# Attention weights summed over four steps in both halves, and the second feed-forward product taken transposed

## The chip, the cores and the metric

The kernel runs on one core of a Trainium2 chip. Time is the device time of one execution in microseconds. Five runs of the kernel before gave 4252.23 to 4266.6 us, with a median of 4262.65 us. A profile is one further execution, recorded instruction by instruction. The engines are TensorE (PE; its weight loads are PEld), VectorE (DVE), ScalarE (ACT), GpSimd (POOL) and SyncE (SP). SP and POOL issue the DMA transfers.

## The reference

Sixteen graphs of 1024 nodes with 256 features pass through four layers, in float32. The graphs share one adjacency matrix. Every layer normalizes its input, clips it at zero, applies a graph layer and adds the result to the input. Layers 0 to 2 are graph attention with 4, 1 and 1 heads. Layer 3 is self-attention with 8 heads of 32 features, masked by the adjacency, followed by a norm, a feed-forward part of two products, and another norm:

```python
attn = softmax(where(mask, q @ k.T / sqrt(32), -1e9))
t = attn @ v
x = layernorm(x + t, ln1_g, ln1_b)
h = relu(x @ w1 + b1)
x = layernorm(x + (h @ w2 + b2), ln2_g, ln2_b)
```

The change touches layer 3 alone: the row sums of the softmax, and the second product.

## The kernel before

**Plan.** `direct` (L301) does the work. Each operation is recorded with its engine, a cost in microseconds, and the buffers that it reads and writes. `Record.schedule` (L170) then runs a list scheduler over the whole program: at each turn it takes the operation that can start earliest, and among those that are ready the one with the smallest key. What comes out is the fixed order of each engine's queue and of the DMA queues of SP and POOL. The hardware follows it with semaphores. The key of an operation is its batch number plus a value read off a curve for its stage (`GATS` for the three graph layers, `VALUES` for the projections of layer 3, `STEPS` for its attention, `FEED` for the feed-forward part), less `LEAD` for ACT and DVE. `BIAS` weighs PE's switching between kinds of matmul. With these curves several batches are in work at once: the feed-forward part of one batch, the attention of a second and the graph layers of later ones are woven into each other. In the steady part a batch takes some 258 us (starts of the scores of batches 4 to 14 in the trace).

**Attention of layer 3** (`attention`, L1029). For each of two head groups `g` (four heads each) and each half `hf` of the query nodes (512 columns) there are eight steps `jt`, one per 128 key nodes. A step computes the scores of four heads on PE (L1297) into the `sc` ring of four PSUM banks, takes the exponential on ACT (L1321) into two tiles `pa` of 1024 columns, and multiplies these by the mask on DVE (L1330). Two steps later (`LAG`) PE multiplies them with the values in a `quad`: four heads side by side, 32 columns each (L1163, `pa,va`). The softmax sums come from another quad with a tile of ones (`sums,ones` or `pa,ones`).

To save quads, the weights of several steps are first added. `run_of` (L1171) says how many: one in the last batch; otherwise four in half 1 and two in half 0. In a run, the second step's tiles are added to the first's by DVE into `sums` (L1190). The third and fourth step's tiles are added into `sums` by DMAs that accumulate, issued on POOL's queue (L1198). `sums` is a ring of two tiles, that is one run at a time; `pa` is a ring of six tiles, that is three steps.

**Projections of queries and keys** (`project`, L1072). Eight times a batch, PE forms a product in an `sc` bank (L1079), ACT copies it rounded to `hi` (L1088), DVE subtracts to get `lo` (L1091), and SP issues 16 DMAs of 64 KB that stack copies of `hi` and `lo` into `qs` or `ks` (L1100). `hi` and `lo` exist once each, so the next projection's copy waits until these DMAs have read them. The table `later` places the projections at steps 0, 2 and 4 of certain halves; those of group 1's first queries and keys are in half 1 of group 0.

**Feed-forward part** (`feed`, L1343), per half: `turn` takes the first norm's statistics on DVE, normalizes `hna` on ACT, transposes it on PE and applies scale and shift on the way out of PSUM (`yT`, ACT L1382). It also scales and shifts the untransposed `hna` on DVE with rows on all partitions (L1397). `forward` forms the first product transposed (L1406) and its relu on ACT into `fz` (L1427). `back`, two node tiles at a time, forms the second product straight, with the weights `w2` moving (L1463); DVE adds `hna` while leaving PSUM and also yields the row sums (L1475, into `z`). Then follow the squares on ACT (L430), a power on POOL (L450), and the scaling and the addition of the layer's input on DVE (L1500, L1513). The result is stored by SP.

**PSUM.** Four banks are the `sc` ring. The other four (`r_bank`) are shared by all else and given out by the plan.

Of the kernel before, what the change touches and what calls it, by code (L numbers as in the profile page):

```python
# [22 lines left out]
P = 128  # L23
# [9 lines left out]
def rows_on_all(ap, n):  # L33

    return bass.AP(tensor=ap.tensor, offset=ap.offset, ap=[[0, P], [1, n]])
# [222 lines left out]


LANDING = 2.8  # L260
BIAS = 1.211
LEAD = {"act": 2.365, "dve": 1.821}

SWITCH = {
    ("full", "col4"): 0.095,
# [16 lines left out]
def tt_us(n):  # L282
    return (n / 0.96 + 73) / 1000


def stt_us(n):
    return (n / 0.96 + 130) / 1000
# [6 lines left out]
def mm_us(n):  # L294
    return 2 * max(2 * n / 2.4 + 2.3, 109) / 1000
# [5 lines left out]
def direct(ctx, tc, flag, x, adj, gat_w, gat_a, w_qkv, ln1_g, ln1_b, ln2_g, ln2_b, w1, b1, w2, b2, out):  # L301
# [9 lines left out]
    HG = P // D3  # L311

    GATS = (
        (-4.564, -3.715, -2.378, -1.791, -0.286),
        (-0.159, 0.648, 0.672, 0.678, 0.719),
        (0.713, 0.729, 0.86, 0.888, 1.159),
    )
    VALUES = (0.885, -0.207, 0.784, 0.867, 1.288)
    STEPS = (0.767, 1.497, 1.58, 1.837, 1.895)
    FEED = (3.303, 2.616, 2.682, 3.025, 3.186)  # L320

    const = ctx.enter_context(tc.tile_pool(name="const", bufs=1))
    ident = const.tile([P, P], F32, name="ident")
# [15 lines left out]
    w1_sb = const.tile([P, CT, C], F32, name="w1_sb")  # L339
    w2_sb = const.tile([P, CT, C], F32, name="w2_sb")  # L340

    cols = {n: const.tile([P, CT], F32, name=f"col_{n}") for n in ("b1", "g1", "c1")}
    rows = {n: const.tile([P, 1, C], F32, name=f"row_{n}") for n in ("g1", "cb", "g2", "c2")}
    mask = const.tile([P, NT, N], U8, name="mask")

    least = const.tile([P, NT], F32, name="least")
# [5 lines left out]
    def ring(name, n, shape, pool=work):  # L352
        return Ring([pool.tile([P] + shape, F32, name=f"{name}{i}") for i in range(n)])
# [24 lines left out]
    r_reca = ring("reca", 1, [CT * 2 * TH * HG])  # L378
    r_mv1 = ring("mv1", 2, [NT, 2])
    r_rstd1 = ring("rstd1", 2, [NT])  # L380
    r_yT = ring("yT", 1, [CT, HALF])
    r_fz = ring("fz", 2, [HALF])
    r_z = ring("z", 2, [HALF])
    r_sums = ring("sums", 2, [2, HALF])
    r_mvz = ring("mvz", 2, [2, 2])
    r_rstdz = ring("rstdz", 2, [2])
# [15 lines left out]
    def pe(us, emit, w, r, modes=("full", "full")):  # L402
        rec.add("pe", us, emit, w, r, modes)
# [4 lines left out]
    def dve(us, emit, w, r):  # L408
        rec.add("dve", us, emit, w, r)
# [233 lines left out]
    def setup():  # L643
        rec.stream(-3.0, (0.0, 1.0), False)
        prepare(0)
        rec.stream(-0.9, (0.0, 0.1), False)
        for it in range(NT):
            neighbours(it)
        rec.stream(-0.5, (0.0, 0.3), False)
        prepare(1)  # L650
        prepare(2)
        dma(
            3.2,
            lambda: nc.sync.dma_start(wqkv_sb, w_qkv.rearrange("(t p) d -> p t d", p=P)),
            [b_qkv],
            [],
        )

        def load_feed():
            nc.sync.dma_start(w1_sb, w1.rearrange("(t p) d -> p t d", p=P))  # L660
            nc.sync.dma_start(w2_sb, w2.rearrange("(t p) d -> p t d", p=P))
            for n, ap in (("b1", b1), ("g1", ln1_g), ("c1", ln1_b)):
                nc.sync.dma_start(cols[n], ap.rearrange("(t p) -> p t", p=P))
            for n, ap in (("g1", ln1_g), ("cb", ln1_b), ("g2", ln2_g), ("c2", ln2_b)):
                nc.sync.dma_start(rows[n][:, 0, :], rows_on_all(ap, C))
            nc.gpsimd.dma_start(rows["cb"][:, 0, :], rows_on_all(b2, C), accum_op=ALU.add)

        dma(5.0, load_feed, [b_feed], [], us=3.6)

# [359 lines left out]
    def attention(b, xt, b_mv, b_rstd):  # L1029
# [140 lines left out]

        def run_of(g, hf):  # L1171

            return 1 if b == NB - 1 else 4 if hf == 1 else 2

        rec.stream(b, STEPS)
        GROUP = 2
# [166 lines left out]
    def feed(b, x3, hn):  # L1343

        mv, rstd = r_mv1.new(), r_rstd1.new()
        yTs, fTs = {}, {}

        def turn(hf):
            s = slice(hf * TH, (hf + 1) * TH)
            its = range(hf * TH, (hf + 1) * TH)  # L1350
            for it in its:
                stats(hn.at(it), hn(it), mv.t[:, it, :], mv(it), "f")
            mv_refs = [mv(it) for it in its]
            inverse(mv.t[:, s, 0], mv.t[:, s, 1], rstd.t[:, s], mv_refs, rstd(hf))
            for it in its:
                u = hn.at(it)
                normal(
                    u,
                    hn(it),
                    u,  # L1360
                    hn(it),
                    mv.t[:, it, 0:1],
                    rstd.t[:, it : it + 1],
                    [mv(it), rstd(hf)],
                    AF.Identity,
                )
            yTs[hf] = r_yT.new()
            for ct in range(CT):
                g = r_bank.new()
                pe(  # L1370
                    0.109 * TH,
                    lambda: transposes(
                        lambda k: g.t[:, k * P : (k + 1) * P],
                        lambda k: hn.half(hf)[:, k, ct * P : (ct + 1) * P],
                        TH,
                    ),
                    [g, yTs[hf](ct)],
                    [hn(it) for it in its],
                )
                act(  # L1380
                    act_us(HALF, 2),
                    lambda: nc.scalar.activation(  # L1382
                        yTs[hf].t[:, ct, :],
                        g.t,
                        AF.Identity,
                        bias=cols["c1"][:, ct : ct + 1],
                        scale=cols["g1"][:, ct : ct + 1],
                    ),
                    [yTs[hf](ct)],
                    [g, b_feed],  # L1390
                )

            h = hn.half(hf)
            for op, row in ((ALU.mult, "g1"), (ALU.add, "cb")):
                dve(
                    tt_us(TH * C),
                    lambda: nc.vector.tensor_tensor(  # L1397
                        h, h, rows[row].to_broadcast([P, TH, C]), op
                    ),
                    [hn(it) for it in its],  # L1400
                    [b_feed],
                )

        def product(g, co, w_sb, src):
            for ct in range(CT):
                nc.tensor.matmul(  # L1406
                    g.t,
                    w_sb[:, ct, co * P : (co + 1) * P],
                    src(ct),
                    start=ct == 0,  # L1410
                    stop=ct == CT - 1,
                )

        def forward(hf):
            yT = yTs[hf]
            fT = fTs[hf] = [r_fz.new() for _ in range(CT)]
            for co in range(CT):
                g = r_bank.new()
                pe(
                    CT * mm_us(HALF),  # L1420
                    lambda: product(g, co, w1_sb, lambda ct: yT.t[:, ct, :]),
                    [g, fT[co]],
                    [yT],
                )
                act(
                    act_us(HALF, 1),
                    lambda: nc.scalar.activation(  # L1427
                        fT[co].t, g.t, AF.Relu, bias=cols["b1"][:, co : co + 1]
                    ),
                    [fT[co]],  # L1430
                    [g],
                )

        def back(hf):
            fT = fTs[hf]
            for it in (hf * TH, hf * TH + 2):
                g, z, mvz, rstdz = r_bank.new(), r_z.new(), r_mvz.new(), r_rstdz.new()
                xr = r_xr.new()
                dma(
                    1.15,  # L1440
# [15 lines left out]
                def pz():  # L1456
                    return g.t.rearrange("p (t c) -> p t c", c=C)

                def product2():
                    for k in range(2):  # L1460
                        i0 = (it % TH + k) * P
                        for ct in range(CT):
                            nc.tensor.matmul(  # L1463
                                pz()[:, k, :],
                                fT[ct].t[:, i0 : i0 + P],
                                w2_sb[:, ct, :],
                                start=ct == 0,
                                stop=ct == CT - 1,
                            )

                pe(2 * CT * mm_us(C), product2, [g], fT)
                for k in range(2):
                    dve(
                        stt_us(C) + 0.03,
                        lambda: nc.vector.scalar_tensor_tensor(  # L1475
                            z_t[:, k, :],
                            pz()[:, k, :],
                            0.0,
                            hn.at(it + k),
                            op0=ALU.add,  # L1480
                            op1=ALU.add,
                            accum_out=mvz.t[:, k, 0:1],
                        ),
                        [z(k), mvz(k)],
                        [g, hn(it + k)],
                    )
                refs = [mvz(0), mvz(1)]
                spread_of(
# [712 lines left out]
```

## Time and profile before

| | before |
|---|---|
| median of 5 runs | 4262.65 us |
| profiled execution | 4254.21 us, span 4252.4 us |
| PE matmul busy | 4086.5 us, 96% |
| DVE busy | 3565.4 us, 84% |
| ACT busy | 2659.8 us, 63% |
| POOL busy | 628.2 us, 15% |
| mean granted PE clock | 0.986 |
| accumulating DMAs `sums<-pa` | 240, 512 KB, 5.9 us from issue to landing (median) |
| projection DMAs to `qs` and `ks` | 2048, 64 KB, 2.0 to 2.1 us |

A group's row in the profile reads: line, engine, operation, output and inputs by the program's names, shapes and count; after the first bar busy time and mean duration in ns; after the second the time its engine stood idle just before, and for whom. A wait reads: who waited for whom, microseconds in total, times, the longest. The chain is the sequence of work that ended last, followed back from the end of the program; its rows give each engine's share of the span. SPq and POOLq are the queues from which DMAs are issued. In a timeline row the first two numbers are start and duration in us. A busy PE is in matmuls whose ends are modelled, so its busy time contains some overlap.

### The profile page before, as it was taken

Reading aid. Unit: us, or ns where it says so; the run is one execution under the profiler, and the core shown is the slowest. Engines: PE = TensorE matmul, PEld = TensorE weight load, DVE = VectorE, ACT = ScalarE, POOL = GpSimd, SP = SyncE. Lnnn points to the kernel's source line nnn. Section 1 sums busy time; section 2 is a strip of 40 time slices with the busy share of each in tenths; the row PEclk is TensorE's granted clock in tenths of the full one; section 3 lists DMA queues with packets and bytes.
Section 4 is the critical chain, followed back from the end, with each engine's and each line's share of the span. In section 5 each row is a group of like instructions: output and inputs, shape, how many; then the busy total and the mean of one; then the engine's idle time right before and its main releaser. Section 6 shows DMA issues by size and latency. Waiting matters only on the chain.

```text
span 4252.4 us, 68427 instructions
## 1 busy us (share of the span) xinstructions
PE 4086.5 (96%) x23874; PEld 2397.1 (56%) x23874; DVE 3565.4 (84%) x6266; ACT 2659.8 (63%) x6383; POOL 628.2 (15%) x632
## 2 busy tenths in 40 slices
PE   7999999999999999999999999999999999999998
PEld 3746556465564645656465564645646456564653
DVE  7487887988889888897988889888898888979877
ACT  3556657665675756657566576666757566575665
POOL 0001111111111111111111111111111111111110
PEclk9999999999999999999999999999999999999999
DMA  3123443343443434443244433334434344332442
GB/s 106 33 67 85 120 98 91 77 97 100 100 104 78 99 84 97 112 93 94 68 99 119 102 87 84 90 102 97 106 74 98 87 97 112 88 89 70 97 113 53
DMA packets 215410, 390.05 MB, mean 92 GB/s; under 512 B 44945, under 2 KB 80401, under 8 KB 215057
## 3 DMA queue, kind: packets, MB, share of 16 engines
q1 hardware_dynamic: 180352, 259.62, 21.8%
q0 software_dynamic: 34704, 125.98, 16.0%
q8 instruction: 191, 3.13, 0.3%
q14 instruction: 163, 1.33, 0.1%
HBM read 91.43 MB, written 33.95 MB: 29 GB/s over the span
## 4 chain that ended last, share of the span: by engine, by line
PE 43%; DVE 20%; ACT 10%; SPq 8%; DMA 6%; issue 4%; POOL 1%; DVEq 0%; ACTq 0%; POOLq 0%
PE bank L842 14%; PE bank L1163 8%; SPq L1100 8%; DVE pt L815 8%; PE sc L1297 6%; DVE pa L1330 5%; PE bank L718 4%; ACT pa L1321 3%; DVE sums L1190 2%; PE bank L513 2%; PE sc L1079 2%; ACT waste L430 2%; PE bank L929 2%; DMA qs<-lo 1%; DMA xt<-in_x_dram 1%
## 5 line engine op out<-in xcount | busy, mean ns | idle before, releaser
L1321 ACT ACTIVATE pa<-sc 128x512 f32<-128x512 f32 x2048 | 1108.7, 602 | 519.0 <-PE sc L1297 323.3
L1330 DVE TENSOR_TENSOR pa<-pa,mask 128x1024 f32<-128x1024 f32 x1024 | 1223.0, 1216 | 97.5 <-ACT pa L1321 94.1
L815 DVE SCALAR_TENSOR_TENSOR pt<-row,e,mask 128x512 f32<-128x512 f32 x1536 | 1063.1, 740 | 33.7 <-DMA row<-rd 24.3
L842 PE MATMUL bank<-qb,pt 128*128 128x257 f32 x4096 | 965.6, 387 | 1.5 <-ACT ex L870 1.0
L842 PEld LDWEIGHTS bank<-qb,pt 128*128 128x128 f32 x4096 | 784.0, 193 | 164.0 <-issue 37.4
L1297 PE MATMUL sc<-qs,ks 128*128 128x512 f32 x2048 | 736.8, 463 | 58.3 <-DVE lo L1091 55.6
L1163 PE MATMUL bank<-pa,va 128*32 128x512 f32 x4096 | 525.4, 597 | 0.7 <-DVE pa L1330 0.7
L1297 PEld LDWEIGHTS sc<-qs,ks 128*128 128x128 f32 x2048 | 368.6, 192 | 273.2 <-ACT pa L1321 74.4
L929 PE MATMUL bank<-pt,qb 128*32 128x512 f32 x4096 | 510.2, 596 | 5.4 <-DVE pt L815 5.4
L1190 DVE TENSOR_TENSOR sums<-pa,pa 128x1024 f32<-128x1024 f32 x360 | 431.0, 1212 | 25.6 <-PE bank L1163 25.5
L718 PE MATMUL bank<-w_aug,hT 128*128 128x259 f32 (+1 forms) x1536 | 390.6, 395 | 2.9 <-ACT hT L712 2.0
L718 PEld LDWEIGHTS bank<-w_aug,hT 128*128 128x128 f32 x1536 | 283.6, 192 | 118.1 <-issue 17.4
L1198 POOL DMA_DIRECT2D sums<-pa x240 | 209.9, 875 | 949.1 <-DVE xt L895 295.2
L929 PEld LDWEIGHTS bank<-pt,qb 128*32 128x32 f32 x4096 | 131.1, 109 | 298.4 <-issue 208.1
L939 PE MATMUL bank<-pt,e 128*32 128x512 f32 x2048 | 285.8, 594 | 0.0
L1163 PEld LDWEIGHTS bank<-pa,va 128*32 128x32 f32 x4096 | 123.8, 109 | 269.9 <-issue 227.7
L870 ACT ACTIVATE ex<-bank,rec 128x256 f32<-128x256 f32 x256 | 120.9, 472 | 209.9 <-DVE rec L862 209.8
L1079 PE MATMUL sc<-hTa,wqkv_sb 128*128 128x512 f32 x512 | 243.7, 604 | 2.1 <-ACT pa L1321 1.9
L484 ACT ACTIVATE hn<-xt,mv,rstd 128x256 f32<-128x256 f32 x384 | 207.7, 609 | 47.1 <-DVE mv L474 31.9
L450 POOL TENSOR_TENSOR rstd<-rstd,neg_half 128x4 f32<-128x4 f32 x94 | 118.0, 1256 | 702.4 <-DVE rstd L442 662.5
L1163 PE MATMUL bank<-sums,ones 128*32 128x512 f32 x1440 | 205.3, 603 | 3.6 <-ACT ex L870 1.9
L430 ACT ACTIVATE waste<-xt,mv 128x256 f32<-128x256 f32 x376 | 191.5, 509 | 9.5
(119 smaller groups left out, 4302.2 us busy)
## 6 DMA issues: line engine op xcount, KB each, us to landing
sums<-pa POOLq DMA_DIRECT2D x240, 512.0 KB, 5.9
row<-rd SPq DMA_DIRECT2D x192, 256.0 KB, 3.2
ks<-hi SPq DMA_DIRECT2D x512, 64.0 KB, 2.1
ks<-lo SPq DMA_DIRECT2D x512, 64.0 KB, 2.0
qs<-hi SPq DMA_DIRECT2D x512, 64.0 KB, 2.0
qs<-lo SPq DMA_DIRECT2D x512, 64.0 KB, 2.0
xt<-in_x_dram SPq DMA_DIRECT2D x32, 512.0 KB, 4.8
x<-xt SPq DMA_DIRECT2D x32, 512.0 KB, 3.2
```

What stands on the lines that cost most here:

```text
L718: nc.tensor.matmul(g.t[:, : C + 3 * H], hT.t[:, ct, k * P : (k + 1) * P], w_aug[l][:, ct, :], start=ct == 0, stop=ct == CT - 1,)
L815: lambda: nc.vector.scalar_tensor_tensor(pt.t, row.t, e3[:, 2, jt // TH, h, jt % TH : jt % TH + 1], mask[:, jt, hf * HALF : (hf + 1) * HAL ...
L842: nc.tensor.matmul(g.t[:, : D + 1], pts[jt].t[:, k * P : (k + 1) * P], qb[:, jt, 0, :], start=jt == 0, stop=jt == NT - 1,)
L929: nc.tensor.matmul(g.t[u * D + d : u * D + d + D3, :], qb[:, j, h + u, d : d + D3], pts[u][j - jt].t, start=j == 0, stop=j == NT - 1,)
L939: nc.tensor.matmul(gd.t[c : c + D3, :], one(jt + k, h + u).to_broadcast([P, D3]), pts[u][k].t, start=jt == 0, stop=jt == NT - 2,)
L1079: nc.tensor.matmul(sc.t, wqkv_sb[:, ct, c0 : c0 + P], hT.t[:, ct, hf * HALF : (hf + 1) * HALF], start=ct == 0, stop=ct == CT - 1,)
L1100: lambda: nc.sync.dma_start(stack.t[a * D3 : (a + 1) * D3, r, at : at + HALF], part.t[r * D3 : (r + 1) * D3, :],),
L1163: nc.tensor.matmul(ac.t[r * D3 : (r + 1) * D3, :], columns(r), of_head(r), start=first, stop=last,)
L1190: lambda: nc.vector.tensor_add(ss.t, p0.t, p1.t),
L1297: nc.tensor.matmul(scs[r - r0].t, ks.t[:, r, jt * P : (jt + 1) * P].bitcast(F32R), q.t[:, r, :].bitcast(F32R), start=True, stop=True,)
L1321: lambda: nc.scalar.activation(pt.t[:, v, :], sc.t, AF.Exp, scale=1.0 / math.sqrt(D3)),
L1330: lambda: nc.vector.tensor_mul(pt.t, pt.t, mask[:, jt : jt + 1, i0 : i0 + HALF].to_broadcast([P, 2, HALF]),),
```

## The change

The sums of the softmax are taken over runs of four steps in both halves. In the feed-forward part the second product is formed transposed, like the first: `w2` is the stationary operand and 512 columns of `fz` move. DVE adds the bias and `yT` while leaving PSUM, back into `yT`. `back` then transposes two node tiles at a time on PE, and ACT copies them from PSUM to `z` and yields the row sums. The untransposed `hna` is no longer scaled and shifted and no longer read by `back`. `yT` gets two buffers, `fz` three, and `z` uses `fz`'s. The rows `g1` and `cb` with their loads go, a column `b2` comes. All numbers of the plan (`BIAS`, `LEAD`, `GATS`, `VALUES`, `STEPS`, `FEED`) are others.

```diff
-BIAS = 1.211
-LEAD = {"act": 2.365, "dve": 1.821}
+BIAS = 1.132
+LEAD = {"act": 2.934, "dve": -1.486}
...
     GATS = (
-        (-4.564, -3.715, -2.378, -1.791, -0.286),
-        (-0.159, 0.648, 0.672, 0.678, 0.719),
-        (0.713, 0.729, 0.86, 0.888, 1.159),
+        (-4.712, -3.106, -1.99, -1.162, 0.152),
+        (0.067, 0.407, 0.645, 0.73, 0.787),
+        (0.795, 0.852, 0.847, 0.891, 1.302),
     )
-    VALUES = (0.885, -0.207, 0.784, 0.867, 1.288)
-    STEPS = (0.767, 1.497, 1.58, 1.837, 1.895)
-    FEED = (3.303, 2.616, 2.682, 3.025, 3.186)
+    VALUES = (0.829, 0.292, 0.735, 1.372, 1.153)
+    STEPS = (1.102, 1.337, 1.602, 1.943, 1.949)
+    FEED = (2.285, 2.308, 2.405, 2.48, 2.233)
...
-    r_yT = ring("yT", 1, [CT, HALF])
-    r_fz = ring("fz", 2, [HALF])
-    r_z = ring("z", 2, [HALF])
+    r_yT = ring("yT", 2, [CT, HALF])
+    r_fz = ring("fz", 3, [HALF])
...
-            for n, ap in (("b1", b1), ("g1", ln1_g), ("c1", ln1_b)):
+            for n, ap in (("b1", b1), ("b2", b2), ("g1", ln1_g), ("c1", ln1_b)):
...
-            for n, ap in (("g1", ln1_g), ("cb", ln1_b), ("g2", ln2_g), ("c2", ln2_b)):
+            for n, ap in (("g2", ln2_g), ("c2", ln2_b)):
...
-            nc.gpsimd.dma_start(rows["cb"][:, 0, :], rows_on_all(b2, C), accum_op=ALU.add)
...
-            return 1 if b == NB - 1 else 4 if hf == 1 else 2
+            return 1 if b == NB - 1 else 4
...
-            h = hn.half(hf)
-            for op, row in ((ALU.mult, "g1"), (ALU.add, "cb")):
-                dve(
-                    tt_us(TH * C),
-                    lambda: nc.vector.tensor_tensor(
-                        h, h, rows[row].to_broadcast([P, TH, C]), op
-                    ),
...
         def forward(hf):
...
+            for co in range(CT):
+                g = r_bank.new()
+                pe(
+                    CT * mm_us(HALF),
+                    lambda: product(g, co, w2_sb, lambda ct: fT[ct].t),
+                    [g],
+                    fT,
+                )
+                u = yT.t[:, co, :]
+                dve(
+                    stt_us(HALF),
+                    lambda: nc.vector.scalar_tensor_tensor(
+                        u, g.t, cols["b2"][:, co : co + 1], u, op0=ALU.add, op1=ALU.add
+                    ),
+                    [yT(co)],
+                    [g],
+                )
...
-                def product2():
+                def turn_back():
                     for k in range(2):
                         i0 = (it % TH + k) * P
-                        for ct in range(CT):
-                            nc.tensor.matmul(
-                                pz()[:, k, :],
-                                fT[ct].t[:, i0 : i0 + P],
-                                w2_sb[:, ct, :],
...
+                        transposes(
+                            lambda ct: pz()[:, k, ct * P : (ct + 1) * P],
+                            lambda ct: yT.t[:, ct, i0 : i0 + P],
+                            CT,
+                        )
...
-                pe(2 * CT * mm_us(C), product2, [g], fT)
+                pe(0.109 * 2 * CT, turn_back, [g], [yT])
                 for k in range(2):
-                    dve(
-                        stt_us(C) + 0.03,
-                        lambda: nc.vector.scalar_tensor_tensor(
...
+                    act(
+                        act_us(C) + 190e-3,
+                        lambda: nc.scalar.activation(
+                            z_t[:, k, :], pz()[:, k, :], AF.Copy, accum_out=mvz.t[:, k, 0:1]
+                        ),
                         [z(k), mvz(k)],
-                        [g, hn(it + k)],
+                        [g],
                     )
```

## The prediction

> **What bounds the kernel now.** I read the page first (busy shares, chain, queues), then the groups by line, then who waits for whom, and last the timeline around the longest wait of TensorE (PE). The profiled execution took 4254.2 us: a span of 4252.4 and 1.8 around it. It lies 8.4 us below the median of the five runs, 4262.65; sums are made on 4254.2, and 8.4 is added at the end. A difference under 0.2% (8.5 us) can't be told from no change here.
>
> ```profile
> PE 4086.5 (96%) x23874; PEld 2397.1 (56%) x23874; DVE 3565.4 (84%) x6266; ACT 2659.8 (63%) x6383; POOL 628.2 (15%) x632
> q1 hardware_dynamic: 180352, 259.62, 21.8%
> q0 software_dynamic: 34704, 125.98, 16.0%
> PE 43%; DVE 20%; ACT 10%; SPq 8%; DMA 6%; issue 4%; POOL 1%; DVEq 0%; ACTq 0%; POOLq 0%
> ```
>
> PE is busy 96%, so its work sets the time, but only 43% of the chain is PE. VectorE (DVE, 84%) and the transfers with their issue (SPq and DMA, 14% together) break in. Queue q0 holds the accumulating DMAs.
>
> ```profile
> L1163 PE MATMUL bank<-sums,ones 128*32 128x512 f32 x1440 | 205.3, 603 | 3.6 <-ACT ex L870 1.9 <-DMA sums<-pa 1.4
> L1190 DVE TENSOR_TENSOR sums<-pa,pa 128x1024 f32<-128x1024 f32 x360 | 431.0, 1212 | 25.6 <-PE bank L1163 25.5
> L1198 POOL DMA_DIRECT2D sums<-pa x240 | 209.9, 875 | 949.1 <-DVE xt L895 295.2 <-DVE reca L1257 168.7 <-DVE sums L1190 122.4
> L1463 PE MATMUL bank<-w_sb,fz 128*128 128x256 f32 x512 | 121.7, 386 | 12.8 <-ACT fz L1427 12.8
> L1406 PE MATMUL bank<-yT,w_sb 128*128 128x512 f32 x256 | 119.7, 593 | 1.3 <-ACT yT L1382 1.3
> L513 PE MATMUL bank<-ident,hn 128*128 128x128 f32 x768 | 116.7, 285 | 12.6 <-ACT hn L484 10.4 <-DVE rec L985 1.0
> L1557 ACT ACTIVATE waste<-xt 128x256 f32<-128x256 f32 x120 | 50.6, 421 | 20.6 <-DMA xt<-in_x_dram 18.8
> ```
>
> These rows are the prices. 1440 matmuls are 180 sums of four heads (8 records each). The accumulating DMAs hardly hold PE: 1.4 us. They act elsewhere:
>
> ```profile
> PE sc L1297 <- DVE lo L1091: 55.6, 17, 6.4
> DVE lo L1091 <- DMA qs<-lo: 48.8, 12, 6.4
> ACT pa L1321 <- DVE sums L1190: 126.3, 60, 5.0
> ACT pa L1321 <- DMA sums<-pa: 7.1, 6, 2.3
> ```
>
> PE's largest wait, 55.6 us in 17 times (about one in each batch), is for `lo`, the low part of a query or key projection, and `lo` waits for the transfers that still read the one `lo` buffer. The timeline of one batch shows why they are late:
>
> ```profile
> 2077.51 4.94 SPq L1100 DMA_DIRECT2D qs<-lo  x8
> ```
> ```profile
> 2128.37 8.21 SPq L1100 DMA_DIRECT2D qs<-lo  x8
> ...
> 2129.26 0.92 POOL L1198 DMA_DIRECT2D sums<-pa  x1 [16.02 <-DVE ota L1264]
> ...
> 2130.61 0.87 POOL L1198 DMA_DIRECT2D sums<-pa  x1
> ...
> 2135.19 0.86 POOL L1198 DMA_DIRECT2D sums<-pa  x1 [3.71 <-DVE pt L815]
> ...
> 2141.88 0.50 PE L1297 MATMUL sc<-qs,ks 128*128 128x512 f32 x1 [3.96 <-DVE lo L1091]
> ```
>
> The same eight issues of SP take 4.94 us with no accumulating DMA about, and 8.21 us when three start during them. Then `lo` is freed late, its subtraction waits at the head of DVE's queue, the score bank it reads stays taken, and PE stands still for 3.96 us.
>
> **The change part by part.**
>
> *Sums of four steps in the first half too.* In 15 batches and 2 head groups, half 0 goes from 4 runs of two to 2 runs of four. PE loses 60 of 180 sums. Four quads back to back last 3.57 us in the chain (0.89 each); busy time gives 205.3/180 = 1.14. So -53.5 to -68; I take -53.5, because a removed quad frees what it occupies between neighbours.
> DVE loses 120 of 360 adds: 120 x 1.212 = -145 us of work. Most lies beside PE. L1190 holds 2% of the chain, some 90 us; a third of it is 30. Bounds 0 to -31; I take -10, since PE itself waits only 0.7 us for masked weights (`pa`). ACT's 126 us of waits for these adds lie in its idle 37%.
> POOL gains 240 x 0.875 = +210 us of issue (15% to 20%). Each issue waits for masked weights; behind it in POOL's queue stand the powers for the norms (L450, L465), for which DVE waits 39.1 + 24.1 + 12.0 = 75 us now. Doubled, and with DVE's 20% of the chain, +15 at most, 0 at least; I take +3, as most of these waits are near the power's own 1 us.
> The landing (5.9 us) must precede the sum; the 1.4 us above price that at 0 to +2, cover being the other groups' products that PE runs meanwhile. If that cover is gone, each of 60 runs would show up to 5.9.
>
> *The transfers.* Accumulating DMAs go from 240 to 480 of 512 KB, q0 from 16% to 32%. SP issues what it issued before in every batch, 128 projection pieces included. The last two steps' accumulations of a run are issued two steps on, so those of half 0's second run start in the first steps of half 1, where queries and keys of the next head group are projected and where PE already stalls. There, eight issues that today pass undisturbed (the `hi` part) would lengthen by the 3.3 us seen above. I price one more stall of today's size in each batch: 15 x 55.6/17 = +49 us. Bounds: 0, if SP issues nothing in the new windows, and +98 for two places. I take +49: of the trace's rows this place is the nearest.
> A rule of the Trainium skill is to be held against this ("DMA: Bandwidth & Descriptors", section "Issuing engines are not separate DMA queues"): DMAs of SP, ACT and POOL end on the same 16 engines and interleave, so POOL's queue is no second road. It speaks against the change and with the 8.21 us. The same page's fit for a POOL DMA ("Anatomy of one DMA") makes 512 KB an estimated 3.2 us; the trace has 5.9, and the trace decides. By 3.2 the disturbance would be 3.2/5.9 of +49, some +27.
>
> *The second feed-forward product, transposed.* PE: 512 matmuls of 256 columns (121.7) become 256 of 512 columns, the shape of L1406 (119.7): -2. Added: 16 transposes per batch, 256 in all. 768 like them are busy 116.7 us (0.152 each, +39); eight in a row in the chain take 0.87 to 1.04 (+28 to +33). I take +36, bounds +28 to +42.
> DVE: 64 scale and shift operations go (39.1 + 38.8 = -78), 128 sums with accumulation go (50.9 + 10.4 = -61), 64 fused adds of 512 from PSUM come. The trace has none; bounds are 0.68 (a product of 512 from PSUM, L992) and 0.74 (L815), so +45. With the adds, DVE falls by some 239 us to 78%. I credit no more than the -10 above: PE does not wait for L1397 or L1475.
> ACT: 128 copies with accumulation, 0.421 + 0.197 each (L1557), +79 us, 63% to 65%. Its idle time hides them; with ACT's 10% of the chain +8 at most.
> At the very end, where nothing covers the feed-forward part, a product (1.7), a fused add (0.7), transposes (0.4) and a slower copy come in, and 2.4 of scale and shift and the straight product (0.9 to 1.7) go: 0, within 3. Setup loads lose a POOL DMA and two broadcasts and gain a small column: 0, hidden by the adjacency work of the first 240 us, within 2.
>
> *Rings and the plan's numbers.* `yT` 2, `fz` 3, `z` gone: 0; PE waits 14 us in all for these tiles. `BIAS`, `LEAD`, `GATS` and the rest reorder everything. No row prices that. A better order can win at most PE's idle time between start and tail: 165.9 less 42 (first 240 us), 17 (last 142 us) and 55.6 for `lo` is 51. I set the loss equally: -51 to +51, taken as 0.
>
> Sum: -53.5 - 10 + 3 + 49 + 36 - 2 = +22.5. 4254.2 + 22.5 = 4276.7; with 8.4, 4285.
>
> **Rivals.**
> *PE's work decides (faster).* The new accumulations fall where SP issues nothing: the +49 is gone, -26.5, 4236. For it: of the present windows only one place per batch stops PE, and half 0's first run could fall between projections. Against: projections follow each other in SP's queue with hardly a gap around that place. It decides from 26 us, about half a stall per batch.
> *Two stalls or a worse order.* Another place of the same kind, or an order that costs +51: 4334 to 4336. For it: q0 at 32% also meets the row broadcasts and the x loads, which are in the chain today. Against: DVE at 78% has more slack.
> *Half of it.* SP's slowing costs about 1.6 us per batch: 4285 - 25 = 4260, no change. For it: the two DMAs of a step overlap.
> *The change doesn't do what it says:* the sums go, but each run ends in a wait for the landing, 60 x 5.9 x one half = +177. Half 1 does the same now and PE waits 1.4 us, so 2 in 100, inside the slower cases.
>
> **How the numbers follow.** Forecast (4285, own range 4268 to 4310) 0.40; two stalls or a worse order 0.20; PE's work decides 0.28; half of it 0.12. Of the forecast's 0.40 some 0.02 lies within 0.2%, of "half" 0.09 does and 0.03 is faster. Faster 0.31, same 0.11, slower 0.58. The range reaches to the faster case with half of the order's gain (4236 - 25, 4210) and to the worse case with a little over (4348).
>
> **What would show it.** After: 960 sum records for `sums` instead of 1440, 240 adds, 480 accumulating DMAs; DVE near 78%, q0 near 32%; PE's waits for `lo` near 105 us instead of 55.6, with SP's issues of `qs` and `ks` longer. The forecast is wrong if `lo` waits stay at 55 or fall: then the time is near 4236. It is also wrong if PE's longest wait is for landed sums, or if PE's busy time does not fall by about 20.

## The result, and the profile after

The changed kernel takes 4247.11 us (median; 4236.88 to 4253.29), the kernel before 4255.4 us over all its runs. The ratio is 0.998, with a 95% interval of 0.9975 to 0.9985: some 8 us faster, at the edge of what can be told here. The forecast was 4285, slower. The time lies inside the range, but the sign was wrong. The profiled execution took 4248.12 us, with a span of 4246.3.

From the page of the changed kernel: busy times and the DMA queues.

```profile
PE 4094.9 (96%) x23394; PEld 2348.6 (55%) x23394; DVE 3373.0 (79%) x5890; ACT 2669.4 (63%) x6639; POOL 788.3 (19%) x871
q0 software_dynamic: 69120, 251.69, 31.4%
q1 hardware_dynamic: 180336, 259.36, 21.6%
```

DVE's busy time fell by 192 us and POOL's rose by 160 us; q0 doubled. PE's busy time *rose* by 8 us. The groups (count; busy and mean; idle before) show why, first the value quads (`pa,va`) of the kernel before, then the changed kernel:

```profile
L1163 PE MATMUL bank<-pa,va 128*32 128x512 f32 x4096 | 525.4, 597 | 0.7 <-DVE pa L1330 0.7
```
```profile
L1161 PE MATMUL bank<-pa,va 128*32 128x512 f32 x4096 | 584.2, 601 | 28.8 <-DVE pa L1328 25.4 <-DVE yT L1430 3.1
L1196 POOL DMA_DIRECT2D sums<-pa x480 | 420.4, 877 | 1540.3 <-DVE pa L1328 533.3 <-DVE sums L1188 188.8 <-PE sc L1295 153.7
L1188 DVE TENSOR_TENSOR sums<-pa,pa 128x1024 f32<-128x1024 f32 x240 | 288.6, 1217 | 29.4 <-PE bank L1161 27.2
L1161 PE MATMUL bank<-sums,ones 128*32 128x512 f32 x960 | 147.7, 603 | 3.4 <-DMA sums<-pa 3.4
L1392 PE MATMUL bank<-fz,w_sb 128*128 128x512 f32 x256 | 124.7, 610 | 0.6 <-ACT fz L1413 0.6
L512 PE MATMUL bank<-ident,yT 128*128 128x128 f32 x256 | 40.6, 283 | 6.6 <-DVE yT L1430 4.1 <-ACT yT L1379 2.4
```

The sums fell from 205.3 to 147.7, the new transposes take 40.6, the second product 124.7 instead of 121.7: together -14 us, near the -19.5 of the forecast. But the value quads, of which there are as many as before and each as long (597 and 601 ns), went from 525.4 to 584.2: they overlap each other less. In part they are stretched by waits: with the new transfers made small in the same order (`f_small0`, below) the group takes 553.5. So PE's busy time does not tell work from waiting inside a group. (The Trainium skill too, "Perfetto Trace Analysis", section "Identifying the Most-Contended Engine", holds the share of matmul busy time for no good measure of how near PE is to its limit. In the rows above the same 4096 matmuls differ by 58.8 us.)

The waits of PE in the changed kernel, then those of DVE for transfers, before and after:

```profile
PE sc L1295 <- DVE lo L1089: 39.6, 24, 3.2
PE bank L1161 <- DVE pa L1328: 25.4, 35, 4.0
```
```profile
DVE xr L1447 <- DMA xr<-x: 36.5, 18, 2.9
...
DVE pt L815 <- DMA row<-rd: 24.3, 21, 4.6
```
```profile
DVE pt L813 <- DMA row<-rd: 99.1, 32, 7.2
...
DVE xr L1450 <- DMA xr<-x: 74.6, 28, 7.3
```

The wait for `lo` did not double; it fell from 55.6 to 39.6 us. DVE's waits for the row broadcasts went from 24.3 to 99.1 and for the load of the layer's input (`xr`) from 36.5 to 74.6.

Three stretches, cut at the first scores of batch 2 and of batch 14 (766.85 and 3867.22 us before, 719.85 and 3823.33 after). Columns: stretch, its length, busy time and count of PE, PEld, DVE, ACT, POOL, mean granted clock of PE, DMA share, GB/s. First before, then after:

```profile
225.00:767.00 542.00, 526.23 (x3140) 301.40 (x3139) 456.85 (x786) 335.33 (x813) 77.98 (x79) 0.99 0.39 92
767.00:3867.00 3100.00, 3020.08 (x17736) 1780.13 (x17736) 2667.60 (x4655) 1986.09 (x4783) 487.37 (x480) 0.99 0.40 94
3867.00:4252.00 385.00, 357.37 (x2030) 198.13 (x2026) 309.38 (x515) 241.03 (x531) 47.24 (x46) 0.98 0.33 80
```
```profile
225.00:720.00 495.00, 484.87 (x2783) 279.65 (x2782) 403.79 (x694) 319.22 (x786) 98.29 (x108) 1.00 0.57 127
720.00:3823.00 3103.00, 3032.11 (x17352) 1749.68 (x17352) 2517.57 (x4369) 1996.08 (x4992) 614.20 (x672) 0.99 0.56 127
3823.00:4246.00 423.00, 387.63 (x2174) 199.45 (x2170) 312.09 (x505) 253.81 (x595) 61.21 (x63) 0.97 0.43 97
```

Twelve batches in the steady part take 3100 us before and 3103 us after: 258.36 and 258.62 us each. Fewer matmuls and less work on DVE brought nothing there. The 6 us of span come from the ends: attention starts some 47 us earlier and the tail is 38 us longer, since more work of other stages is left over.

### The profile page after: what moved, and what is told of

Its sections match the earlier page's. It is cut to its first block, busy times and chain, and to the rows that moved or that the text cites. A ratio compares the mean times of both kernels' runs of the same rounds, so it can differ in the third digit from the quotient of the medians.

```text
span 4246.3 us, 67947 instructions
## 1 busy us (share of the span) xinstructions
PE 4094.9 (96%) x23394; PEld 2348.6 (55%) x23394; DVE 3373.0 (79%) x5890; ACT 2669.4 (63%) x6639; POOL 788.3 (19%) x871
## 3 DMA queue, kind: packets, MB, share of 16 engines
q0 software_dynamic: 69120, 251.69, 31.4%
## 5 line engine op out<-in xcount | busy, mean ns | idle before, releaser
L1328 DVE TENSOR_TENSOR pa<-pa,mask 128x1024 f32<-128x1024 f32 x1024 | 1220.9, 1215 | 82.3 <-ACT pa L1319 80.0
L813 DVE SCALAR_TENSOR_TENSOR pt<-row,e,mask 128x512 f32<-128x512 f32 x1536 | 1063.6, 741 | 111.8 <-DMA row<-rd 99.1
L1295 PE MATMUL sc<-qs,ks 128*128 128x512 f32 x2048 | 712.2, 453 | 42.7 <-DVE lo L1089 39.6
L1196 POOL DMA_DIRECT2D sums<-pa x480 | 420.4, 877 | 1540.3 <-DVE pa L1328 533.3
L1161 PE MATMUL bank<-pa,va 128*32 128x512 f32 x4096 | 584.2, 601 | 28.8 <-DVE pa L1328 25.4
L927 PE MATMUL bank<-pt,qb 128*32 128x512 f32 x4096 | 525.6, 596 | 6.5 <-DVE pt L813 5.8
L1188 DVE TENSOR_TENSOR sums<-pa,pa 128x1024 f32<-128x1024 f32 x240 | 288.6, 1217 | 29.4 <-PE bank L1161 27.2
L937 PE MATMUL bank<-pt,e 128*32 128x512 f32 x2048 | 301.6, 592 | 0.0
L464 POOL TENSOR_TENSOR rstd<-rstd,neg_half 128x4 f32<-128x4 f32 x66 | 128.6, 1949 | 692.2 <-DVE rstd L461 686.1
L449 POOL TENSOR_TENSOR rstd<-rstd,neg_half 128x4 f32<-128x4 f32 x94 | 122.2, 1300 | 719.4 <-DVE rstd L441 719.4
L958 ACT COPY ot<-bank 128x512 f32<-128x512 f32 x128 | 71.6, 582 | 212.5 <-PE bank L927 157.0
```

Of the source, the lines that this page charges most:

```text
L813: lambda: nc.vector.scalar_tensor_tensor(pt.t, row.t, e3[:, 2, jt // TH, h, jt % TH : jt % TH + 1], mask[:, jt, hf * HALF : (hf + 1) * HAL ...
L927: nc.tensor.matmul(g.t[u * D + d : u * D + d + D3, :], qb[:, j, h + u, d : d + D3], pts[u][j - jt].t, start=j == 0, stop=j == NT - 1,)
L937: nc.tensor.matmul(gd.t[c : c + D3, :], one(jt + k, h + u).to_broadcast([P, D3]), pts[u][k].t, start=jt == 0, stop=jt == NT - 2,)
L1161: nc.tensor.matmul(ac.t[r * D3 : (r + 1) * D3, :], columns(r), of_head(r), start=first, stop=last,)
L1188: lambda: nc.vector.tensor_add(ss.t, p0.t, p1.t),
L1196: lambda: nc.gpsimd.dma_start(ss.t, pt.t, accum_op=ALU.add),
```

## The experiments

Two kinds are used. In the first, what an instruction does is cut down while its planned cost stays, so the order of every engine and queue is that of the kernel it is taken from (in `f_skip` one small reduction on DVE near the end stands elsewhere); only the duration or size differs. In the second, the edits are made one at a time, and the planner makes a new order for each. Ratios are to the kernel before, run beside them.

### The same order, less work on PE or DVE

Two of four sums quads in half 0 left out (`f_skip`); in `f_add` half of the adds narrowed; in `f_both` both.

```diff
+                    left_out = run == 2 and jt in (3, 5)
-                        lambda: quad(
+                        lambda: None if left_out else quad(
...
...
+                    few = run == 2 and jt in (3, 7)
...
+                        return t[:, 0, :16] if few else t
...
-                            lambda: nc.vector.tensor_add(ss.t, p0.t, p1.t),
+                            lambda: nc.vector.tensor_add(part(ss.t), part(p0.t), part(p1.t)),
```

> The kernel before in its own order of every engine, but two of the four sums quads in half 0 (after steps 3 and 5) are left out, 60 quads in all, so the softmax sums of half 0 lack those steps. Nothing else moves. Theory 'PE sets the time': 60 quads at 0.855 to 0.97 us each come off the time, 4255 - 51 to - 58 = about 4200. Theory 'waits set the time' (PE is busy 96% but what it waits for would be waited for anyway): less than 15 us come off, 4240 or more.

> As before, but only the adds are narrowed (120 of them to 16 of 1024 columns); all quads stay. Theory 'DVE holds the steps of half 0': 20 to 50 us come off. Rival: within 10 us of 4256.

> The kernel before in its own order; in half 0 two of four sums quads are left out (60 quads) and half of the adds on DVE take only 16 of 1024 columns (120 adds, some 137 us of DVE), so the softmax sums of half 0 are incomplete. This is what runs of four take away, without the transfers that they bring. The quads alone gave 0. Theory 'DVE holds the steps of half 0': 30 to 60 us come off, 4200 to 4225. Theory 'the transfers of half 1 with SP's queue set the period': within 10 us of 4256.

Measured: `f_skip` 0.9998 (0.9989 to 1.0007), `f_add` 0.9983 (0.9975 to 0.9992), `f_both` 0.996 (0.9945 to 0.9976). Sixty quads, 51 us of pure matmul time on an engine that is 96% busy, are worth nothing in this order. PE's first wait in `f_skip`:

```profile
PE sc L1298 <- DVE lo L1091: 59.0, 16, 6.3
PE bank L513 <- DVE z L1476: 24.2, 14, 1.8
```

PE came earlier to where it waits anyway; the second line is a wait that the kernel before hardly had. Both cuts together give 17 us, between the two theories' ranges. So the theory that PE's work sets the time falls for this order, and the theory that DVE holds the steps of half 0 holds for a small part only.

### The same order, small transfers

All 240 accumulating DMAs of the kernel before cut to 16 columns (`f_small_b`); in the changed kernel only the 240 new ones of half 0 (`f_small0`).

```diff
-                            lambda: nc.gpsimd.dma_start(ss.t, pt.t, accum_op=ALU.add),
+                            lambda: nc.gpsimd.dma_start(part(ss.t), part(pt.t), accum_op=ALU.add),
```

> The kernel before in its own order, but all 240 accumulating DMAs add only 16 of 1024 columns, so the softmax sums of half 1 lack nearly all of the third and fourth steps. Issues on POOL and all waits stay. Theory 'the transfers slow SP's issues and PE pays': the 55.6 us of waits for lo go, about 4255 - 50 = 4205. Rival 'that wait is the plan's own': lo waits stay above 35 us and the time within 15 us of 4255.

> The changed kernel in its own order, but the 240 accumulating DMAs of half 0 (the new ones) add only 16 of 1024 columns, so the softmax sums of half 0 lack nearly all of the third and fourth steps. Theory 'the new transfers ate the gain of PE's work': 4247 - 15 to - 40 = 4207 to 4232, with DVE's waits for row (99 us) back near 24. Rival 'the order ate it': within 8 us of 4247.

Measured: `f_small_b` 0.9656 (0.9643 to 0.9668), 4110.65 us; `f_small0` 0.9874 (0.9859 to 0.9888), 4201.0 us against 4247.11 of the changed kernel. The bytes of the old accumulations cost 146 us, three times what I had expected; those of the new ones 46 us. SP's queue in `f_small_b`, at the place of the stall shown in the prediction:

```profile
2064.75 4.99 SPq L1100 DMA_DIRECT2D qs<-lo  x8
```

The eight issues take 4.99 us instead of 8.21, and PE's wait for `lo` is gone from the list of its longest waits. Whether a plain transfer of that size, one that doesn't accumulate, would slow SP's issues as much was not tried. Over the whole trace of the kernel before, the 395 projection issues that begin within 5 us of an accumulating issue take 1.04 us on average, the other 1653 take 0.60; in `f_small_b` it is 0.59 and 0.60. The two traces have the same instructions in the same order, so their times can be subtracted one by one: of the 9.3 us that a batch is shorter, 4.1 arise at the scores that wait for `lo`, the rest in pieces of up to 1.2 us behind it.

Part of the rest is a second cost of the stall, which no list of waits holds. Right after the 3.96 us stall shown in the prediction, PE's granted clock is 0.50 for 3.4 us. There the matmuls of L842 start 0.43 us apart, elsewhere 0.22. In the columns of the stretches above, this place and then the steady part of the kernel before, and last the steady part of `f_small_b`:

```profile
2143.20:2146.60 3.40, 3.40 (x10) 2.65 (x9) 3.40 (x6) 1.52 (x4) 2.63 (x1) 0.50 0.57 130
226.00:3949.00 3723.00, 3627.20 (x21383) 2121.98 (x21381) 3202.55 (x5560) 2371.19 (x5701) 577.45 (x567) 0.99 0.39 93
```
```profile
226.00:3949.00 3723.00, 3698.58 (x22074) 2188.58 (x22073) 3312.63 (x5773) 2467.96 (x5917) 640.12 (x593) 1.00 0.25 64
```

In the trace of the kernel before, between 226 us and the last 300 us, the clock is halved 16 times, 75.1 us in all; each time begins within 5 us of the end of a pause of PE of 2.3 to 6.4 us. In `f_small_b` PE has no pause of over 2 us there, and the clock is never halved. Half of 75.1, some 37 us of the 146, is an estimate of what comes this way; no run separates the pauses from the halved clock.

For the new transfers the subtraction points elsewhere. In 14 batches the changed kernel loses 2.2 to 5.1 us (2.6 in the median, 39 in all) at one instruction of DVE, the addition of `ln2_b` to the loaded input. The timeline of the changed kernel, then of `f_small0`:

```profile
2074.22 0.39 SPq L1515 DMA_DIRECT2D out_dram<-xr  x1
...
2075.81 0.90 POOL L1196 DMA_DIRECT2D sums<-pa  x1 [0.27 <-ACT pa L1319]
...
2078.60 0.88 POOL L1196 DMA_DIRECT2D sums<-pa  x1 [0.49 <-DMA sums<-pa]
...
2079.06 0.32 SPq L1444 DMA_DIRECT2D xr<-x  x1
...
2082.49 0.69 DVE L1450 TENSOR_TENSOR xr<-xr,row_c 128x512 f32<-128x512 f32 x1 [3.45 <-DMA xr<-x]
...
2085.87 0.62 PE L1161 MATMUL bank<-pa,va 128*32 128x512 f32 x2 [0.60 <-DVE pa L1328]
```
```profile
2054.20 0.39 SPq L1520 DMA_DIRECT2D out_dram<-xr  x1
...
2056.36 0.32 SPq L1449 DMA_DIRECT2D xr<-x  x1
...
2059.24 0.69 DVE L1455 TENSOR_TENSOR xr<-xr,row_c 128x512 f32<-128x512 f32 x1 [0.22 <-DMA xr<-x]
```

The ring `xr` has two tiles, so a load waits until the store of the tile's last content has landed. Beside accumulations the load is issued 4.84 us after the store's issue instead of 2.16, and the addition starts 3.43 us after that instead of 2.88. DVE waits 3.45 us for the load at the head of its queue, the masked weights behind it are late, and PE's value quads wait for them. The sums of these waits say the same, in the changed kernel and then, with the group of the value quads, in `f_small0`:

```profile
SPq L1444 <- DMA out_dram<-xr: 160.7, 47, 6.9
```
```profile
SPq L1449 <- DMA out_dram<-xr: 83.0, 47, 5.9
...
DVE pt L813 <- DMA row<-rd: 92.7, 31, 4.6
...
DVE xr L1455 <- DMA xr<-x: 36.9, 27, 4.1
...
L1161 PE MATMUL bank<-pa,va 128*32 128x512 f32 x4096 | 553.5, 599 | 9.4 <-DVE pa L1333 5.9 <-DVE yT L1435 3.2
```

DVE's wait for `xr` falls from 74.6 to 36.9 us. Its wait for the rows stays at 92.7, where I had expected about 24; so that wait belongs to the new order and not to the size of the new transfers.

### That wait taken away

`f_noc2` is the changed kernel in its own order without that operation; the load stays. `v_xr` is a complete kernel: the load's planned time goes from 1.15 to 4.4 us, and the planner makes a new order.

```diff
 f_noc2:
-                    lambda: nc.vector.tensor_add(
-                        xr.t, xr.t, rows["c2"].to_broadcast([P, 2, C])
-                    ),
+                    lambda: None,
 v_xr:
                 dma(
-                    1.15,
+                    4.4,
                     lambda: nc.sync.dma_start(xr.t, x3.t[:, it : it + 2, :]),
```

> The changed kernel in its own order without the operation on DVE that adds ln2_b to the loaded input (L1450), so ln2_b is left out of the output. The load and all else stay. In the traces with and without the new transfers, the same instruction comes 3.2 us later in each batch at this operation alone, waiting for its load. Theory 'the new transfers cost through this wait': the 46 us come off, 4247 - 40 to - 55 = 4192 to 4207. Rival 'DVE meets the same delay one instruction later' (row, lo or masked weights): within 15 us of 4247.

> The changed kernel with the load of the layer's input for the last addition planned at 4.4 us instead of 1.15, so that the planner puts the operation that waits for it later. It orders anew. If that wait is the price of the new transfers and the order stays as good otherwise: 4200 to 4225. If a new order by itself moves the time by tens of us: anything from 4215 to 4300.

Measured: `f_noc2` 0.9836 (0.9817 to 0.9854), 4187.74 us; `v_xr` 0.9854 (0.9835 to 0.9872), 4194.66 us. Without the operation 59 us come off, a little more than expected. The operation's own 43.9 us of DVE are probably only a small part of that: 137 us less of DVE gave 7 us in `f_add`, though at another place. With the 39 us of the subtraction, this shows that the 46 us of the new transfers are paid mostly here. The same operation left out of `f_small0`, where it waits half as long, would have helped to tell its own price; that was not run. `v_xr` beats both kernels, by 1.5% and 1.2%. Its waits:

```profile
PE sc L1295 <- DVE lo L1089: 16.6, 10, 2.2
```
```profile
DVE xr L1450 <- DMA xr<-x: 33.0, 14, 3.1
```

The wait for `xr` more than halved; but that for `lo`, with which the edit has nothing to do, fell as well, since the order is another. The halved clock, too, falls from 65 to 25 us after the first 226 us. Two more runs were to tell the one from the other: the same 4.4 in the kernel before (`v_xr_b`), and rows planned longer too (`v_xr_row`).

```diff
 v_xr_row, besides 4.4 for xr:
             dma(
-                1.4,
+                4.0,
                 lambda: nc.sync.dma_start(
                     row.t,
```

> The kernel before with the same one number changed (the load for the last addition planned at 4.4 us instead of 1.15). In its trace DVE waits 36.5 us for this load and PE hardly pays for it. If the gain of the changed kernel with 4.4 came from the wait for the load: little here, 4235 to 4256. If a new order by itself moves the time by tens of us: outside of 4225 to 4285.

> The changed kernel with that load at 4.4 us and the broadcasts of rows planned at 4.0 us instead of 1.4; DVE still waits 85 us for rows with the load at 4.4 alone (4195). If planning transfers at what they take beside accumulations helps in general: 4150 to 4185. If it was this one wait: 4185 to 4205. If a new order by itself decides: above 4215.

Measured: `v_xr_b` 1.0044 (1.0029 to 1.0059), `v_xr_row` 1.0324 (1.0307 to 1.0341). The first, 4272.72 us, lies between its two expectations: the number did not help the kernel before, as it should not if the wait matters in the changed kernel alone, but it cost some 18 us, clear of noise, by the new order. So it does not tell the two apart. The second refutes that planning transfers longer helps in general: 199 us are lost against `v_xr` by one more number. How much of `v_xr`'s gain is the wait and how much a lucky order stays open; that this wait costs the changed kernel some 40 us is shown by the subtraction and by `f_noc2`, in which the order is the same.

### The edits one by one

Runs of four in half 0, the transposed product with its rings, and the plan's numbers, each old or new:

```diff
 c_run4, on the kernel before:
-            return 1 if b == NB - 1 else 4 if hf == 1 else 2
+            return 1 if b == NB - 1 else 4
 c_plan, on the kernel before: BIAS, LEAD, GATS, VALUES, STEPS, FEED of the changed one
 c_prod, on the changed kernel: those numbers and run_of of the one before
 c_feed, on the changed kernel:
-    FEED = (2.285, 2.308, 2.405, 2.48, 2.233)
+    FEED = (3.303, 2.616, 2.682, 3.025, 3.186)
```

> The kernel before with runs of four in half 0 as the only change; the plan's numbers and the straight product stay, the planner orders anew. PE does 60 quads less, DVE 120 adds less, 240 accumulating DMAs more. Theory 'PE's work decides': 4255 - 50 = 4205. Theory 'the new transfers eat the gain': 4245 to 4265. Theory 'the order decides': anything from 4215 to 4300, with PE's quads for pa,va waiting for masked weights.

> The transposed second product alone (with its rings), on the plan's old numbers and runs of two in half 0. Runs of four alone cost 34 us, so product and plan's numbers together must have brought some 42. Theory 'the product brings it', by 94 us less work on DVE: 4256 - 42 = about 4215. Theory 'the plan's numbers bring it': 4250 to 4275, as PE gains 28 us of transposes.

> Both edits of the work, runs of four in half 0 and the transposed product, on the plan's old numbers. Theory 'the product brings it': 4247, as the changed kernel. Theory 'the plan's numbers bring it': 4290 or more, as with runs of four alone.

> The changed kernel with runs of two in half 0. If runs of four cost their 34 us here too: 4247 - 34 = 4213. If the plan's new numbers suit runs of four, so that the edits depend on each other: 4247 or more.

> Runs of four in half 0 and the plan's new numbers, with the straight product. Theory 'the plan's numbers bring it': 4247. Theory 'the product brings it': 4290.

> The plan's new numbers alone: runs of two in half 0, straight product. So far, against 4255: runs of four alone +34, product alone +162, both +132; with the new numbers, product with runs of two +90, runs of four with straight product +16, all three -8. If the new numbers are simply better by some 70 to 140 us whatever the work: 4115 to 4185. If each set of numbers fits only the work that it stands beside: 4255 or more, as high as 4340.

> The changed kernel with only the FEED curve set back to the old numbers (the feed-forward part about one batch later in the order). If FEED is what made the transposed product bearable: 4350 to 4387, as with all old numbers. If it is another of the numbers or their sum: within 40 us of 4247.

| half 0 | second product | plan's numbers | ratio (95%) | us |
|---|---|---|---|---|
| two | straight | old | 1 (before) | 4255.4 |
| four | straight | old (`c_run4`) | 1.0086 (1.0073 to 1.0099) | 4290.3 |
| two | transposed | old (`c_prod`) | 1.0379 (1.0365 to 1.0393) | 4417.56 |
| four | transposed | old (`c_run4_prod`) | 1.0316 (1.0301 to 1.033) | 4386.92 |
| two | straight | new (`c_plan`) | 1.0282 (1.0265 to 1.0299) | 4377.35 |
| four | straight | new (`c_run4_plan`) | 1.0045 (1.0031 to 1.0058) | 4271.73 |
| two | transposed | new (`c_prod_plan`) | 1.0211 (1.0197 to 1.0224) | 4345.56 |
| four | transposed | new | 0.998 (0.9975 to 0.9985) | 4247.11 |
| four | transposed | new, old `FEED` (`c_feed`) | 1.0369 (1.035 to 1.0387) | 4412.47 |

No edit has a price of its own. Runs of four cost 35 us under the old numbers with the straight product and bring 98 us under the new ones with the transposed. The new numbers cost 122 us for the old work and bring 140 us for the new. Each set of numbers suits the work beside which it stands; every mixture is slower than both whole kernels, and `FEED` alone decides 165 us. Counted from the records of ten middle batches, the matmuls' own cadence takes 235.7 us of a batch before, 234.0 after, 237.4 in `c_prod` and 236.2 in `c_plan`. What is left of the period is 22.9, 24.9, 34.4 and 31.2 us: changes between kinds of matmul, waits, and what the halved clock costs (estimated as half of its time: 2.6, 1.9, 4.3 and 1.9 us). The work differs by 3 us among these kernels, the rest by 12.

### Sums without accumulating DMAs

If the transfers cost so much, the sums could be had without them: runs of two in both halves on the kernel before (`v_run2_b`), or GpSimd adding in place of the DMAs in the changed kernel (`v_pool_a`).

```diff
 v_run2_b:
-            return 1 if b == NB - 1 else 4 if hf == 1 else 2
+            return 1 if b == NB - 1 else 2
 v_pool_a:
-                        dma(
-                            3.0,
-                            lambda: nc.gpsimd.dma_start(ss.t, pt.t, accum_op=ALU.add),
+                        pool(
+                            2.3,
+                            lambda: nc.gpsimd.tensor_tensor(
+                                out=ss.t, in0=ss.t, in1=pt.t, op=ALU.add
+                            ),
```

> The kernel before with runs of two in both halves: no accumulating DMA at all, 120 adds more on DVE (+145 us), 60 quads more on PE (+51 us of matmuls). Accumulations of half 1 cost 146 us in the kernel before. Theory 'that is all transfers': 4256 - 146 + 51 to + 100 = 4160 to 4210. Rival 'DVE at 87% becomes the bound': 4256 or more.

> The changed kernel with the third and fourth step's tiles added by GpSimd (a tensor_tensor add of 1024 columns, planned at 2.3 us) in place of the 480 accumulating DMAs. No trace shows GpSimd's price for this shape. If it takes 2 to 3 us and disturbs nobody: 4247 - 46 to - 120 = 4130 to 4200. Rival 'GpSimd slows DVE or is late': 4260 or more.

Measured: `v_run2_b` 1.021 (1.0197 to 1.0223), `v_pool_a` 1.1857 (1.1841 to 1.1873). Runs of two lose 88 us. PE's wait for `lo` shrank to 11.6 us, but work and order took more than that; which of the two was not separated. GpSimd's add is dear in itself and makes DVE slower:

```profile
L1328 DVE TENSOR_TENSOR pa<-pa,mask 128x1024 f32<-128x1024 f32 x1024 | 1499.1, 1491 | 112.0 <-ACT pa L1319 112.0
L1196 POOL TENSOR_TENSOR sums<-sums,pa 128x1024 f32<-128x1024 f32 x480 | 1474.9, 3089 | 1198.5 <-DVE pa L1328 566.6 <-DVE sums L1188 311.1 <-DVE rec L860 193.9
```

The masking takes 1491 ns on average instead of 1215, with a median of 1218 and a longest of 3425: most are untouched, and the longest last as long as a GpSimd add and more. That fits the Trainium skill ("SBUF — State Buffer", section "Terms": DVE and GpSimd share a port pair, and the loser blocks entirely). The clock is halved here as well, for 584 us after the first 226 us against 65 in the changed kernel: by the same estimate some 260 of the 795 us that this kernel loses to it.

## Why the prediction was right or wrong

- *PE's work, -19.5 us.* The size was nearly right as busy time: -57.6 for the sums (-53.5 foreseen), +40.6 for the transposes (+36), +3 for the product (-2), in all -14. Its worth was wrong, at least for the sums. "PE is busy 96%, so its work sets the time" is refuted by `f_skip`: the same number of quads gone in the old order changed nothing.
- *DVE, -10 us.* Within its bounds: 7 us for the adds alone and 17 with the quads, in the old order.
- *POOL and ACT, +3 and 0.* No wait of PE for ACT grew by more than 7 us, and none for POOL is in its list; not tried by itself.
- *The new transfers, +49 us.* The size was right, 46 us in the same order. The place was wrong: not one more stall for `lo`, whose wait fell, but DVE waiting for the `xr` load, which the changed order had put beside the new accumulations. That the size fits is thus partly luck. The mechanism is half the one foreseen: a transfer late beside accumulations and an engine waiting for it at the head of its queue; but what was late is the landing of a store before a load, not a row of SP's issues.
- *The plan's numbers, "-51 to +51, taken as 0".* This is the step that failed. The sum prices the new work at +22.5 us and lets the numbers change nothing. On the old numbers the new work costs +131.5 us (`c_run4_prod`), and the new numbers take 140 us off again. The bound took PE's recorded idle time as all that an order can win, and set the loss equal to it. But much of what an order costs is hidden in PE's busy time, as changes between kinds of matmul, pauses within groups and the halved clock; and an order made for other work can lose far more than 51 us (`c_plan`: 122). The -8 us are the difference of larger terms, of which +46 is the one shown in the changed order itself; that they cancel to within 40 us of the forecast is luck.
- *The 8.4 us added at the end.* The median of 47 runs of the kernel before is 4255.4, so the profiled execution's 4254.2 was close to it; the addition was too much.
- *Rivals.* The faster one came nearest in time (4236), but for another reason: the new accumulations did fall where others issue, and they cost 46 us.
- *What would show it.* Counts, DVE (79%) and q0 (31.4%) were as stated. "`lo` waits stay at 55 or fall: then the time is near 4236" held within 11 us, for the wrong reason. The other sign, that PE's busy time does not fall by about 20, came true as well: it rose by 8.

## What to carry to other kernels

Where a planner fixes the order of every queue, don't price an edit to the work apart from the plan's numbers that come with it: here the order was worth 140 us, against 14 us of PE's busy time. To learn what one thing costs, keep its planned cost and shrink what it does; two traces in the same order can then be subtracted instruction by instruction, and they show the place that lists of waits only hint at. Look among the waits for transfers whose planned time is too short, above all where an engine waits for them at the head of its queue; but measure each new number, since it makes a new order: of three tries here one won 52 us and two lost. And read the granted clock beside the waits: after a pause PE may run slower for a while.

## What the runs showed of the hardware

- An accumulating DMA from SBUF to SBUF (512 KB, 5.5 to 5.9 us to landing in the median) slows the issue of 64 KB DMAs on SP's queue from 0.60 to 1.04 us on average in the 5 us after its own issue, though it is issued on POOL; with 16 columns instead of 1024 nothing is slowed (0.59). The 240 of them cost 146 us of 4255.
- 51 us of matmul time taken from a PE that the profile calls 96% busy changed the time by 0.0% (`f_skip`).
- In the kernel before, each of the 16 times that PE's granted clock fell to half in the steady part, for 3.4 to 10.2 us, began within 5 us of the end of a pause of PE of 2.3 to 6.4 us. `f_small_b`, without a pause over 2 us there, has no such time.
- A GpSimd add of 128x1024 float32 takes 3.09 us on average beside DVE's work, 2.33 at the shortest, against DVE's 1.21; and some DVE operations beside it last up to 3.4 us instead of 1.22.
